# Two GNN layers on one core: fewer weights and q loads ahead of the attention loop, and another layout of the tiles that live longest there

## The chip, the cores and the metric

The kernel runs on one core of a Trainium2 chip. The metric is the device time of one execution in microseconds (us). TensorE appears in the profile as PE (and PEld for its weight loads), VectorE as DVE, ScalarE as ACT, GpSimd as POOL, SyncE as SP. SP, ACT and POOL can issue DMAs; "SPq" is SP's queue, "ACTq" that of ACT. L12 means line 12 of the kernel before.

## What is computed

There are 3327 nodes with 128 features, and a dense adjacency matrix. Cut to what matters:

```python
h = relu(layernorm(x))                                  # layer 0
agg = adj.T @ h / deg
x = x + relu(batchnorm(agg @ W_n.T + b_n + h @ W_c.T + b_c))

h = relu(layernorm(x))                                  # layer 1, n=3327, d=128, 8 features each
q = (h @ Wq.T).reshape(d, n, 8)                         # the same for k and v
a = einsum('dnh,dmh->dnm', q, k) * d**-0.5 + adj + adj
out = einsum('dnm,dmh->dnh', softmax(a, axis=2), v)
x = x + out.reshape(n, 8 * d) @ Wo.T
```

Layer 1 is 128 attentions over all 3327 nodes with eight features each; they are nearly all of the work.

## The kernel before

All instructions are placed by hand: each engine runs its own in the order of the program text, and the framework inserts the waits. Where a tile takes memory that an earlier tile held, its first user waits for the last users of the earlier one. Pools lie on a stack: pools opened after a closed one get its memory.

**Layer 0 (L286 to L598)**, about 300 us. The adjacency is read in 26 chunks (L412), and PE sums the seven `acc` banks. The nodes `x` live in `xs`, the normed nodes of layer 1, turned, in `B`; `A` and `C` are work tiles of the same size. All four are in the pool `l0`, `xs` first. Three chunks' buffers (`l0adj`) then take the last seven columns' worth of the transposed adjacency for the first three query blocks (`EARLY = 3`, L433). `weigh_early` (L439) turns such a buffer into weights exp(2 adj) with one ACT instruction and writes it to DRAM (`wd`). It runs twice beside the batch norm (L499) and once at the end (L598).

After the batch norm, `residual` adds the layer's output to `xs` for four chunks of nodes at a time and writes these to DRAM (`xd`); `stats` takes their layer-norm statistics. The first part of q, k and v is projected early (`project_now`, L567) and written to DRAM. SP then loads k (8 loads of 208 KB) and v, and ACT issues 16 loads of q (104 KB each, all 3328 columns). Then, in the order of the text: casts of k into place, alternately on POOL and ACT (L581); the rest of the residuals; `roots(4, NC)` on ACT (L591); the norms, turns and columns of layer 1 into `B`; `hd`, the write of `B` to DRAM (L597); the last `weigh_early`.

**Between (L647).** A pool `zero` with a small tile `zeros`, set by POOL and written by a POOL DMA behind the end of `att`.

**Layer 1, the loop (L652 to L869).** 32 batches `i` of four attentions, 7 blocks `y` of queries (six of 512, one of 255), 13 steps `s`: 2912 steps. A step handles four pieces of keys. For two or three of them ("plain") PE forms the scores, DVE adds the adjacency (L818, tile `d` from `at`, read from DRAM), ACT takes the exponential of all of them (L856). For one or two pieces ("rest") ACT takes the exponential straight from PSUM (L828) and POOL multiplies by the ready weights `wt` (L831, read from `wd`). PE then sums with v (L604), three steps later (`LAG`). `fetch` loads `at` (four buffers) and `wt` (three) two steps ahead.

In the first batch, `more_weights` (L734) makes the weights of block y + 1 during block y, but only from block 3 on (`y + 1 < EARLY` returns): four times a load `t`, an exponential on ACT a step later (L749) and a write to `wd` a step after that. `beside` runs further projections there, on PE, DVE and POOL, using the tile `ov`. From step 39 of the first batch the q, k and v of the next batch are loaded into the second set of tiles.

Of the kernel before, what the change touches and what calls it, by code (L numbers as in the profile page):

```python
# [9 lines left out]
F32 = mybir.dt.float32  # L10
# [5 lines left out]
PSUM = bass.MemoryType.PSUM  # L16
DRAM = bass.MemoryType.DRAM

N = 3327
D = 128  # L20
H = 8
P = 128
NC = 26
T = N * D
NP = NC * P
NB = 512
G = 4
# [4 lines left out]
WC = 19  # L32
CH = 4 * NP // D
NG = D // G
EARLY = 3

# [6 lines left out]
def tile_two_layer_gnn(  # L45
# [17 lines left out]
    nc = tc.nc  # L63
# [4 lines left out]
    blocks = [(n0, min(NB, N - n0)) for n0 in range(0, N, NB)]  # L68

    const = ctx.enter_context(tc.tile_pool(name="const", bufs=1))  # L70
# [6 lines left out]
    qT = dram.tile([2 * H, TP], F32, name="qT")  # L77
# [5 lines left out]
    att = dram.tile([TP, H], F32, name="att")  # L83

    wd = dram.tile([NC - WC, P, N], F32, name="wd")
    xd = dram.tile([NP, D], F32, name="xd")
# [9 lines left out]
    make_identity(nc, ident)  # L96
    ones = const.tile([P, P], F32, name="ones")
    nc.vector.memset(ones, 1.0)
    eps = const.tile([P, 1], F32, name="eps")
    nc.vector.memset(eps, EPS)  # L100
    wqk = [const.tile([P, H * D], F32, name=n) for n in ("wq", "wk", "wv")]
# [5 lines left out]
    low_half = const.tile([P, 2], F32, name="low_half")  # L107
# [18 lines left out]

    sets = [tile_set(x) for x in range(2)]

    def q_loads(q, p0, d):

        qs = qT[:, bass.ds(d * N, NP)].rearrange("(a h) n -> a h n", h=H)
        return [(q[p0 + i * H : p0 + (i + 1) * H].bitcast(F32), qs[i // 2]) for i in range(4)]

    def k_loads(k, p0, d, n0, n):
        cols = bass.ds(d * N + n0, n)
# [101 lines left out]
    def projections(wk, hj, j, quick, ov, factor):  # L237
        return [
            projection(wk, hj, j, s, e, quick, ov, factor) for s in (1, 0, 2) for e in range(2)
        ]  # L240
# [45 lines left out]
    with tc.tile_pool(name="l0", bufs=1) as l0, tc.tile_pool(  # L286
        name="l0adj", bufs=3
    ) as ap, tc.tile_pool(name="l0s", bufs=2) as sp, tc.tile_pool(
        name="l0p", bufs=1, space=PSUM
    ) as pp:  # L290
        xs = l0.tile([P, NC, D], F32, name="xs")
        A = l0.tile([P, NC, D], F32, name="A")
        B = l0.tile([P, NC, P], F32, name="B")
        C = l0.tile([P, NC, P], F32, name="C")
        A2, B2, C2 = (t.rearrange("p c d -> p (c d)") for t in (A, B, C))
        junk = l0.tile([P, N], mybir.dt.bfloat16, name="junk")
# [74 lines left out]
        def beside(x):  # L371

            if x < NQ:
                pt, cs = turned(x, A, aside)
                nc.scalar.copy(B[:, cs, :], pt)
            elif x < 2 * NQ:
# [35 lines left out]
        for c in range(NC):  # L412
            a = ap.tile([P, 7 * NB], F32, name="a")
# [15 lines left out]
            i = c - 2 * NQ - 5  # L429
            if 0 <= i < NQ - 2 and 4 * i + 4 <= c:  # L430
                spread(i)
        weights = []
        for y, (n0, w) in enumerate(blocks[:EARLY]):  # L433
            a = ap.tile([P, 7 * NB], F32, name="a")
            a7 = a.rearrange("p (c n) -> p c n", c=7)
            nc.sync.dma_start(a7[:, :, :w], adjr[:, WC:, n0 : n0 + w])
            weights.append((a7, n0, w))

        def weigh_early():  # L439
            a7, n0, w = weights.pop(0)  # L440
            nc.scalar.activation(a7[:, :, :w], a7[:, :, :w], AF.Exp, bias=low, scale=2.0)
            nc.sync.dma_start(
                wd[:, :, n0 : n0 + w].rearrange("c p n -> p c n"), a7[:, :, :w]
            )
# [6 lines left out]
        b = l0.tile([1, 6], F32, name="bound")  # L451
# [37 lines left out]
        for i, (n0, w) in enumerate(blocks):  # L489
            s = slice(n0, n0 + w)  # L490
            nc.vector.tensor_tensor(B2[:, s], acc[i][:, :w], B2[:, s], ALU.mult)
            nc.tensor.matmul(acc[i][:, :w], wn, B2[:, s], start=True, stop=True)
            if i >= 1:
                hidden(i - 1)
            if i in (0, 2):
                spread(NQ - 2 + i // 2)
            if i == 3:
                set_flag()
            if i in (4, 6):  # L499
                weigh_early()  # L500
        hidden(NQ - 1)
        nc.vector.bn_aggr(bmv, bst.rearrange("p i s -> p (i s)"))
# [9 lines left out]
        def relu(i):  # L512
            n0, w = blocks[i]
            s = slice(n0, n0 + w)
            nc.scalar.activation(A2[:, s], A2[:, s], AF.Relu, bias=shift, scale=scale)

        def residual(i):
            pt, cs = turned(i, A, acc[i])
            nc.vector.tensor_add(xs[:, cs, :], xs[:, cs, :], pt)
            nc.sync.dma_start(  # L520
                xd.rearrange("(c p) d -> p c d", p=P)[:, cs, :], xs[:, cs, :]
            )

        def second_norm(i, engine):

# [6 lines left out]
        def columns(i, scalar):  # L532
            pt, cs = turned(i, C, acc[i])
            if scalar:
                nc.scalar.activation(B[:, cs, :], pt, AF.Relu)
            else:
                nc.vector.tensor_scalar(B[:, cs, :], pt, 0.0, None, ALU.max)

        def keep_columns(i0, i1):
            s = slice(4 * i0 * P, min(NC, 4 * i1) * P)  # L540
            nc.sync.dma_start(hd[:, s], B2[:, s])

        ov0 = l0.tile([P, D, H + 1], F32, name="ov0")
        nc.gpsimd.memset(ov0, 1.0)

        def project_now(j, banks):
            todo = projections(sp, B2[:, j * CH : (j + 1) * CH], j, True, ov0, low_half[:CH, 1:2])
            for p, b in zip(todo, banks):
                drive(p, b)
            for p in todo:  # L550
                drive(p)
                drive(p)
# [16 lines left out]
        q, k, v = sets[0]  # L569
        ks = sets[1][1].rearrange("p c n -> p (c n)")  # L570
# [4 lines left out]
            nc.sync.dma_start(*args)  # L575
        for i in range(4, NQ):
            relu(i)
        for b in range(G):
            for args in q_loads(q, 32 * b, b):
                nc.scalar.dma_start(*args)  # L580
        for x, c in enumerate(range(0, NC, 4)):  # L581
            n = min(4, NC - c)
            (nc.scalar.copy if x % 2 else nc.gpsimd.tensor_copy)(
                k[:, c : c + n, :],
                ks.bitcast(F32).rearrange("g (p c) -> g c p", c=NC)[:, c : c + n, :],
            )
        for i in range(2, NQ):
            if i > 2:
                residual(i)
# [4 lines left out]
            second_norm(i, nc.gpsimd if i % 3 == 0 else nc.vector)  # L594
        for i in range(1, NQ):
            columns(i, i % 2 == 0)
        keep_columns(0, NQ)  # L597
        weigh_early()  # L598

# [41 lines left out]
    def rows_of(c):  # L643
        return min(P, N - c * P)


    with tc.tile_pool(name="zero", bufs=1) as zp:  # L647
        z = zp.tile([P, H], F32, name="zeros")
        nc.gpsimd.memset(z, 0.0)
        nc.gpsimd.dma_start(att[T:, :], z)  # L650

    def attention():  # L652


        with tc.tile_pool(name="adj", bufs=4) as ap, tc.tile_pool(
            name="adw", bufs=3
        ) as wp, tc.tile_pool(name="exd", bufs=4) as ep, tc.tile_pool(
            name="exf", bufs=5
        ) as fp, tc.tile_pool(
            name="res", bufs=2  # L660
        ) as rp, tc.tile_pool(name="wk", bufs=2) as wk, tc.tile_pool(
            name="wk1", bufs=1
        ) as wk1, tc.tile_pool(name="psc", bufs=3, space=PSUM) as psc, tc.tile_pool(
            name="pav", bufs=1, space=PSUM
        ) as pav:

# [1 line left out]
            avs2 = [pav.tile([P, NB], F32, name=f"av{x}") for x in range(2)]  # L668
            for av in avs2:
                nc.vector.memset(av, 0.0)  # L670
            ov = wk1.tile([P, D, H + 1], F32, name="ov")
            nc.gpsimd.memset(ov, 1.0)
            if True:
                steps = [
                    (i, y, s)
# [16 lines left out]
                for x, (i, y, s) in enumerate(steps):  # L692
                    n0, w = blocks[y]
# [4 lines left out]
                    c = pairs(s)[1][0][0]  # L698
# [30 lines left out]
                    return p  # L729

                waiting, ending, pending = [], [], []
                late = None

                def more_weights(i, y, s):  # L734

                    k, phase = s // 3, s % 3
                    if i or y + 1 >= len(blocks) or y + 1 < EARLY or k > 3:
                        return
                    n0, w = blocks[y + 1]
                    c = WC + 2 * k  # L740
                    n = min(2, NC - c)
                    if phase == 0:
                        have["w"] = wk.tile([P, 2, NB], F32, name="t4")
                        nc.sync.dma_start(
                            have["w"][:, :n, :w], adjr[:, c : c + n, n0 : n0 + w]
                        )
                    elif phase == 1:
                        a = have["w"][:, :n, :w]
                        nc.scalar.activation(a, a, AF.Exp, bias=low, scale=2.0)  # L749
                    else:  # L750
                        nc.sync.dma_start(
                            wd[c - WC : c - WC + n, :, n0 : n0 + w].rearrange("c p n -> p c n"),
                            have["w"][:, :n, :w],
                        )
# [44 lines left out]
                for x, (i, y, s) in enumerate(steps):  # L799
                    n0, w = blocks[y]  # L800
                    fetch(x + PRE)
                    k = x - i * SU * len(blocks) - FROM[i]
# [4 lines left out]
                    while pending and (total - len(pending)) * (SU * len(blocks) - FROM[i] - 4) <= k * total:  # L807
                        pending.pop(0)()
                    more_weights(i, y, s)
                    due = len(waiting) == LAG  # L810
                    plain, rest = pairs(s)
                    d = ep.tile([P, 3, 2, NB], F32, name="d")
# [251 lines left out]
```

## Time and profile before

| | us |
|---|---|
| median of 3 runs (10511.46 to 10516.91) | 10513.71 |
| the profiled execution, its own time | 10527.91 |
| its span, from first to last instruction | 10526.1 |
| core clock granted to TensorE, mean | 0.986 |
| DMA: mean rate over the span | 165 GB/s |

The page also divides the span into 40 slices of 263 us (each digit is a busy share in tenths). The first slice holds layer 0, the rest is the loop:

```profile
PE   7889999999999999999999999999999999999999
DVE  5789999999999999999999999999999999999998
ACT  4889999999999999999999999999999999999998
POOL 0667777777777777777777777777777777777776
```

Later quotations are of two kinds. Lines of groups give line, engine, operation and tiles, then count, busy time and mean ns, then idle time before them and what ended it. Lines of a timeline give start and duration in us, then the instruction; in brackets stands the idle time of the engine before it.

### The profile page before, as it was taken

What the parts mean: (1) busy time and instruction counts of PE and PEld (TensorE: products, weight loads), DVE (VectorE), ACT (ScalarE), POOL (GpSimd) and SP (SyncE); (2) the same over time, 40 slices, a digit from 0 to 9 for tenths busy, and PEclk for the clock granted to TensorE, in tenths of its full rate; (3) what the DMA queues carried; (4) which work ended last, traced back from release to release, by engine and by line L of the source; (5) the groups of instructions that cost most, each with busy time, mean ns of one, the idle gap of its engine ahead of it and who ended that gap; (6) DMA issues with size and microseconds to landing.
All of it is one profiled execution on the core that took longest, in us unless ns stands there. A gap on an engine that the chain in (4) does not pass through costs nothing. (4 is left out here: it accounts for less than half of the span.)

```text
span 10526.1 us, 186778 instructions
## 1 busy us (share of the span) xinstructions
PE 9922.7 (94%) x72399; PEld 2813.8 (27%) x72399; DVE 9714.9 (92%) x9949; ACT 9948.5 (95%) x6200; POOL 7497.1 (71%) x3868
## 2 busy tenths in 40 slices
PE   7889999999999999999999999999999999999999
PEld 3222222222222222222222222222222222222222
DVE  5789999999999999999999999999999999999998
ACT  4889999999999999999999999999999999999998
POOL 0667777777777777777777777777777777777776
PEclk8899999999999999999999999999999999999999
DMA  7655555555555555555555555555555555555554
GB/s 241 192 168 163 157 168 165 163 162 160 162 166 165 164 162 157 161 170 163 160 162 157 165 170 165 160 158 163 164 169 163 162 163 158 165 165 167 156 152 128
DMA packets 1115761, 1731.67 MB, mean 165 GB/s; under 512 B 198350, under 2 KB 441932, under 8 KB 1107180
## 3 DMA queue, kind: packets, MB, share of 16 engines
q1 hardware_dynamic: 1110478, 1713.99, 56.3%
q8 instruction: 568, 9.31, 0.4%
q10 hardware_dynamic: 4350, 5.64, 0.2%
q14 instruction: 333, 2.73, 0.1%
q0 software_dynamic: 32, 0.00, 0.0%
HBM read 1618.76 MB, written 100.53 MB: 163 GB/s over the span
## 5 line engine op out<-in xcount | busy, mean ns | idle before, releaser
L818 DVE SCALAR_TENSOR_TENSOR d<-at,s 128x1024 f32<-128x1024 f32 x8512 | 9204.3, 1138 | 642.7 <-PE s L725 406.2
L831 POOL TENSOR_TENSOR f<-f,wt 128x1024 f32<-128x1024 f32 (+1 forms) x3136 | 6983.8, 2235 | 2619.1 <-ACT f L828 2572.0
L856 ACT ACTIVATE d<-d 128x3072 f32<-128x3072 f32 (+1 forms) x2912 | 7372.9, 2532 | 73.4 <-DVE d L818 70.5
L604 PE MATMUL av<-d,v 128*9 128x512 f32 x34048 | 5528.5, 569 | 0.1
L725 PE MATMUL s<-q,k 32*128 32x512 f32 x23296 | 4280.7, 482 | 505.7 <-DVE d L818 218.0
L725 PEld LDWEIGHTS s<-q,k 32*128 32x128 f32 x23296 | 1773.9, 182 | 5829.2 <-DVE d L818 3312.2
L828 ACT ACTIVATE f<-s 128x1024 f32<-128x1024 f32 (+1 forms) x3136 | 3014.8, 970 | 313.8 <-PE s L725 252.3
L604 PE MATMUL av<-f,v 128*9 128x512 f32 x12544 | 2864.0, 571 | 0.0
L604 PEld LDWEIGHTS av<-d,v 128*9 128x9 f32 x34048 | 630.7, 88 | 1381.6 <-issue 1265.4
L604 PEld LDWEIGHTS av<-f,v 128*9 128x9 f32 x12544 | 310.6, 88 | 52.9 <-issue 41.0
L180 POOL CAST k<-ks 128x256 fp32r<-128x256 f32 x434 | 284.2, 655 | 0.0
L416 PE MATMUL acc<-a,A 128*128 128x512 f32 (+1 forms) x364 | 151.3, 568 | 24.0 <-ACT A L350 23.3
L619 PEld LDWEIGHTS av<-ident,avs 128*128 128x128 f32 (+1 forms) x864 | 121.1, 208 | 179.9 <-issue 178.8
L226 POOL TENSOR_TENSOR o<-pf,o 104x512 fp32r<-104x512 f32 x124 | 160.4, 1293 | 9.9
L619 PE MATMUL av<-ident,avs 128*128 128x128 f32 (+1 forms) x864 | 163.8, 311 | 0.6 <-DVE avs L612 0.6
L225 POOL CAST o<-pf 104x512 fp32r<-104x512 f32 x124 | 75.8, 611 | 115.3 <-DVE pf L224 59.8
L612 DVE COPY avs<-av 128x512 f32<-128x512 f32 (+1 forms) x224 | 144.2, 644 | 2.8 <-PE av L604 2.8
L423 DVE TENSOR_REDUCE amax<-a 128x1 f32<-128x3327 f32 x26 | 93.7, 3610 | 37.7 <-DMA a<-in_adj 37.7
L416 PEld LDWEIGHTS acc<-a,A 128*128 128x128 f32 x364 | 68.8, 192 | 108.8 <-issue 84.4
L420 ACT ACTIVATE junk<-a 128x3327 bf16<-128x3327 f32 x26 | 77.4, 2977 | 6.6 <-DMA a<-in_adj 6.5
L389 POOL TENSOR_TENSOR sq<-wk 128x512 f32<-128x512 f32 x2 | 2.1, 1040 | 102.3 <-PE aside L390 102.3
L629 DVE TENSOR_TENSOR oq<-av,ri 128x128 f32<-128x128 f32 (+1 forms) x224 | 64.1, 286 | 7.7
(120 smaller groups left out, 952.0 us busy)
## 6 DMA issues: line engine op xcount, KB each, us to landing
at<-in_adjT SPq DMA_DIRECT2D x1728, 512.0 KB
wt<-wd SPq DMA_DIRECT2D x1344, 256.0 KB
at<-in_adjT SPq DMA_DIRECT2D x288, 255.0 KB
ks<-kT SPq DMA_DIRECT2D x496, 104.0 KB
q<-qT SPq DMA_DIRECT2D x496, 104.0 KB
at<-in_adjT SPq DMA_DIRECT2D x192, 256.0 KB
a<-in_adj SPq DMA_DIRECT2D x26, 1663.5 KB
wt<-wd SPq DMA_DIRECT2D x224, 127.5 KB
```

The lines of the kernel that those rows point to most:

```text
L180: nc.gpsimd.tensor_copy(k[:, c : c + n, half * 64 : half * 64 + 64], ks.bitcast(F32).rearrange("g (p c) -> g c p", c=NC)[:, c : c + n, :],)
L226: nc.gpsimd.tensor_tensor(o[:CH, 1], f[:CH], o[:CH, 0].bitcast(F32), ALU.subtract)
L416: nc.tensor.matmul(acc[i][:, :w], A[:, c, :], a[:, n0 : n0 + w], start=(c == 0), stop=(c == NC - 1),)
L423: nc.vector.tensor_reduce(amax[:, c : c + 1], a[:, :N], AX.X, ALU.max, apply_absolute_value=True)
L604: nc.tensor.matmul(av[32 * b : 32 * b + H + 1, :w], tiles[2][:, b, c, :], e, start=first, stop=last,)
L612: nc.vector.tensor_copy(avs[:, :w], av[:, :w])
L619: nc.tensor.transpose(pt[:R, j, :], avs[:, j : j + (R - 1) * J + 1 : J], ident)
L725: nc.tensor.matmul(p[:, x, :we], k[rs, c, :], q[rs, n0 : n0 + we], start=True, stop=True,)
L818: nc.vector.scalar_tensor_tensor(d[:, j, :, :w], have[0, i, y, c // 2][:, c % 2, :w] .unsqueeze(1).to_broadcast([P, 2, w]), SAFE / 2, p[:, ...
L828: nc.scalar.activation(f[:, :, :w], p[:, :, :w], AF.Exp, scale=2.0)
L831: nc.gpsimd.tensor_tensor(f[:, :, :w], f[:, :, :w], have[1, i, y, c][:, :w].unsqueeze(1).to_broadcast([P, 2, w]), ALU.mult,)
L856: nc.scalar.activation(flat, flat, AF.Exp, scale=2.0)
```

## The change

Seven edits belong together.

1. `EARLY` goes: only block 0 gets its weights ahead of the loop (one `weigh_early`, at L499). `more_weights` makes those of blocks 1 and 2 in blocks 0 and 1 of the first batch.
2. ACT issues 16 q loads of 512 columns (16 KB each). The rest of the columns (2816, 88 KB each) is loaded by SP, two loads per step in the first eight steps of the loop.
3. The casts of k move from ahead of the residuals to the end of layer 0.
4. `xd` is written once, for all nodes, right before `hd`, in place of seven writes.
5. `xs` and `B` move to a pool `l0last` that lies last on the stack. The loop's pools are reordered so that `exd` and `res` lie there.
6. `zeros` becomes a constant tile, set and written out at the start; the pool `zero` goes.
7. `ov` becomes one constant tile for layer 0 and the loop, set once at the start.

The block size `NB` stays 512.

```diff
-EARLY = 3
...
+    ov = const.tile([P, D, H + 1], F32, name="ov")
+    nc.gpsimd.memset(ov, 1.0)
+    zeros = const.tile([P, H], F32, name="zeros")
+    nc.gpsimd.memset(zeros, 0.0)
+    nc.gpsimd.dma_start(att[T:, :], zeros)
...
-    def q_loads(q, p0, d):
-
-        qs = qT[:, bass.ds(d * N, NP)].rearrange("(a h) n -> a h n", h=H)
-        return [(q[p0 + i * H : p0 + (i + 1) * H].bitcast(F32), qs[i // 2]) for i in range(4)]
+    def q_loads(q, p0, d, n0=0, n=NP):
+
+        qs = qT[:, bass.ds(d * N + n0, n)].rearrange("(a h) n -> a h n", h=H)
+        return [
+            (q[p0 + i * H : p0 + (i + 1) * H, n0 : n0 + n].bitcast(F32), qs[i // 2])
+            for i in range(4)
+        ]
...
-        name="l0p", bufs=1, space=PSUM
-    ) as pp:
-        xs = l0.tile([P, NC, D], F32, name="xs")
+        name="l0last", bufs=1
+    ) as ll, tc.tile_pool(name="l0p", bufs=1, space=PSUM) as pp:
+
+
+        xs = ll.tile([P, NC, D], F32, name="xs")
         A = l0.tile([P, NC, D], F32, name="A")
-        B = l0.tile([P, NC, P], F32, name="B")
+        B = ll.tile([P, NC, P], F32, name="B")
...
-        for y, (n0, w) in enumerate(blocks[:EARLY]):
+        for y, (n0, w) in enumerate(blocks[:1]):
...
-            if i in (4, 6):
+            if i == 4:
                 weigh_early()
...
             nc.vector.tensor_add(xs[:, cs, :], xs[:, cs, :], pt)
-            nc.sync.dma_start(
-                xd.rearrange("(c p) d -> p c d", p=P)[:, cs, :], xs[:, cs, :]
-            )
...
-        ov0 = l0.tile([P, D, H + 1], F32, name="ov0")
-        nc.gpsimd.memset(ov0, 1.0)
...
         for b in range(G):
-            for args in q_loads(q, 32 * b, b):
+            for args in q_loads(q, 32 * b, b, 0, NB):
                 nc.scalar.dma_start(*args)
-        for x, c in enumerate(range(0, NC, 4)):
-            n = min(4, NC - c)
-            (nc.scalar.copy if x % 2 else nc.gpsimd.tensor_copy)(
-                k[:, c : c + n, :],
-                ks.bitcast(F32).rearrange("g (p c) -> g c p", c=NC)[:, c : c + n, :],
-            )
...
         for i in range(1, NQ):
             columns(i, i % 2 == 0)
+        nc.sync.dma_start(xd.rearrange("(c p) d -> p c d", p=P), xs)
         keep_columns(0, NQ)
-        weigh_early()
+        for x, c in enumerate(range(0, NC, 4)):
+            n = min(4, NC - c)
+            (nc.scalar.copy if x % 2 else nc.gpsimd.tensor_copy)(
+                k[:, c : c + n, :],
+                ks.bitcast(F32).rearrange("g (p c) -> g c p", c=NC)[:, c : c + n, :],
+            )
...
-    with tc.tile_pool(name="zero", bufs=1) as zp:
-        z = zp.tile([P, H], F32, name="zeros")
-        nc.gpsimd.memset(z, 0.0)
-        nc.gpsimd.dma_start(att[T:, :], z)
...
-        ) as wp, tc.tile_pool(name="exd", bufs=4) as ep, tc.tile_pool(
+        ) as wp, tc.tile_pool(name="wk", bufs=2) as wk, tc.tile_pool(
             name="exf", bufs=5
-        ) as fp, tc.tile_pool(
+        ) as fp, tc.tile_pool(name="exd", bufs=4) as ep, tc.tile_pool(
             name="res", bufs=2
-        ) as rp, tc.tile_pool(name="wk", bufs=2) as wk, tc.tile_pool(
-            name="wk1", bufs=1
-        ) as wk1, tc.tile_pool(name="psc", bufs=3, space=PSUM) as psc, tc.tile_pool(
+        ) as rp, tc.tile_pool(name="psc", bufs=3, space=PSUM) as psc, tc.tile_pool(
...
-            ov = wk1.tile([P, D, H + 1], F32, name="ov")
-            nc.gpsimd.memset(ov, 1.0)
...
+                others = [
+                    args for b in range(G)
+                    for args in q_loads(sets[0][0], 32 * b, b, NB, NP - NB)
+                ]
...
-                    if i or y + 1 >= len(blocks) or y + 1 < EARLY or k > 3:
+                    if i or y + 1 >= len(blocks) or k > 3:
                         return
...
                     more_weights(i, y, s)
+                    for args in others[:2]:
+                        nc.sync.dma_start(*args)
+                    del others[:2]
```

More of the change, by code (lines that the diff above doesn't have):

```diff
@@ L541, in keep_columns @@
             nc.sync.dma_start(hd[:, s], B2[:, s])
-        ov0 = l0.tile([P, D, H + 1], F32, name="ov0")
-        nc.gpsimd.memset(ov0, 1.0)
         def project_now(j, banks):
-            todo = projections(sp, B2[:, j * CH : (j + 1) * CH], j, True, ov0, low_half[:CH, 1:2])
+            todo = projections(sp, B2[:, j * CH : (j + 1) * CH], j, True, ov, low_half[:CH, 1:2])
             for p, b in zip(todo, banks):
```

## The prediction

> **What bounds the kernel now.** I read the page first, for the engines and the slices; then the windows, to see where the even part begins; then the timeline of the engines between 200 and 320 us, since the change touches that part; last the timeline of ACT in the first blocks of the loop.
>
> The page shows a kernel with three engines nearly full, and one group per engine that fills it:
>
> ```profile
> PE 9922.7 (94%) x72399; PEld 2813.8 (27%) x72399; DVE 9714.9 (92%) x9949; ACT 9948.5 (95%) x6200; POOL 7497.1 (71%) x3868
> L856 ACT ACTIVATE d<-d 128x3072 f32<-128x3072 f32 (+1 forms) x2912 | 7372.9, 2532 | 73.4 <-DVE d L818 70.5
> L828 ACT ACTIVATE f<-s 128x1024 f32<-128x1024 f32 (+1 forms) x3136 | 3014.8, 970 | 313.8 <-PE s L725 252.3
> ```
>
> ACT's two exponentials follow one another without a gap in a step of the loop (ACT's timeline has L828 at 406.54 and the next one at 410.10, so a full step is 3.56 us). In the loop ACT sets the pace, and what is added to ACT there is paid nearly one to one. The change leaves the steady loop alone. It acts on what lies ahead of the first step and on blocks 0 and 1 of the first of 32 batches. So I need two sums: how much earlier the first step starts, and what the first two blocks give back.
>
> Windows (us, then PE, PEld, DVE, ACT and POOL busy, clock, DMA share, GB/s) of the stretch ahead of the loop:
>
> ```profile
> 233.50:264.00 30.50, 0.66 (x4) 0.26 (x2) 6.72 (x38) 0.00 (x0) 0.01 (x1) 0.50 0.80 123
> 264.00:280.00 16.00, 4.98 (x22) 4.22 (x22) 6.14 (x21) 4.91 (x7) 7.08 (x10) 0.52 0.48 102
> 280.00:298.00 18.00, 1.72 (x8) 0.76 (x8) 1.29 (x3) 5.73 (x4) 1.93 (x3) 0.58 0.67 249
> ```
>
> For 64 us hardly any engine works. The timeline (start, duration, what; in brackets the idle time before and what ended it) says why:
>
> ```profile
> 233.49 18.34 SPq L573 DMA_DIRECT2D k<-kT  x8
> 233.77 36.48 ACTq L580 DMA_DIRECT2D q<-qT  x16
> 240.06 0.30 DVE L333 BATCH_NORM_AGGREGATE ln_mv<-ln_st 128x2 f32<-128x6 f32 x2
> 252.76 6.05 SPq L575 DMA_DIRECT2D v<-v  x3
> 270.30 3.25 ACT L583 CAST k<-k 128x512 fp32r<-128x512 f32 x3 [37.39 <-DMA xd<-xs]
> 273.45 0.31 ACT L338 ACTIVATE ln_sd<-ln_mv,eps 128x22 f32<-128x22 f32 x1
> ...
> 280.39 0.34 SPq L541 DMA_DIRECT2D hd<-B  x1
> 281.45 3.28 ACT L441 ACTIVATE a<-a,low_half 128x3584 f32<-128x3584 f32 x1
> 286.29 0.10 POOL L649 MEMSET zeros<- 128x8 f32 x1 [8.63 <-issue]
> 292.04 0.75 POOL L650 DMA_DIRECT2D att<-zeros  x1 [5.64 <-issue]
> 293.97 0.37 SPq L713 DMA_DIRECT2D at<-in_adjT  x1
> 298.15 2.35 DVE L818 SCALAR_TENSOR_TENSOR d<-at,s 128x1024 f32<-128x1024 f32 x2 [16.55 <-DMA at<-in_adjT]
> 300.27 1.02 ACT L828 ACTIVATE f<-s 128x1024 f32<-128x1024 f32 x1 [7.58 <-PE s L725]
> ```
>
> First knot: ACT issues 16 loads of q and needs 36.48 us for it; the root L338, whose statistics were ready at 240.36, is queued behind them and behind ACT's three casts of k, and runs at 273.45. Second knot: `hd<-B` goes out at 280.39; the POOL memset of `zeros`, which takes over the memory of `xs`, starts at 286.29, right when that transfer would be over (5.9 us; the profile says only "issue"), its DMA at 292.04, and the first `at` of the loop, which takes the memory of `zeros`, at 293.97. The wait view puts 8.1 us of SP down to `att<-zeros`. So the first add of the loop starts at 298.15.
>
> **What the Trainium skill says.** "DMA: Bandwidth & Descriptors", section "Issuing engines are not separate DMA queues": loads issued from ScalarE and SyncE run on the same 16 DMA engines and interleave. The trace agrees: the 16 q and 8 k loads share 123 GB/s while the DMA share is 0.80. "Queues, rings and completion order" in the same page says that one DMA is split over up to 16 rings, not always all; here q loads have 8 rows and k loads 16. No view here shows single DMA engines. "ScalarE: Activation LUTs", "What ACT_TABLE_LOAD costs": about 1283 ns, and the trace shows 1.28 us. "TensorE: Matmul & The Clock Gate", Part 1: after idling the array runs at half rate; the trace grants 0.50 to 0.58 in these windows. The start of the loop has that penalty before and after.
>
> **Part 1, up to the root L338.** One exponential of `weigh_early` (two took 6.46 us) leaves ACT in front of the batch-norm roots; the statistics it meets come at 213.45, so only some 0.6 us is won. Without one `wd` write (1792 KB) and three `xd` writes ahead of `kT`, ACT's waits for `kT<-o` (2.53 and 1.04 us) should shrink by about 0.4. The loads thus start 1 us earlier, at 232.5.
>
> The 16 q loads now carry 512 of 3328 columns: 16 KB, not 104. In 233.5 to 264 the core moved 123 GB/s x 30.5 us = 3.75 MB. What must pass now ahead of ACT's last issue is k (8 x 208 KB), v (468 KB) and q (256 KB): 2.44 MB. At the old rate that ends at 252; at 200 GB/s (a block of the loop with loads of this kind runs at 212) at 245; the floor is the statistics, 240. I take 247.5 for the root, since the last q loads were interleaved with the v loads before, and I expect ACT to wait for those. Gain 26 us (21 to 33). The casts of k, moved behind the columns, no longer stand in front of it.
>
> **Part 2, from the root to the first add.** Root to `hd` was 280.39 - 273.45 = 6.94 us (normalising, turning, columns), unchanged. From `hd` to the first add was 17.76 us. Gone from it are `zeros`, its DMA and POOL's `ov` memset; the last exponential and its `wd` write too (ACT's first L828 waited 6.93 us for that write). What is left: `hd` itself (5.9) and one `at` (4.2 from issue to add, 293.97 to 298.15). Wholly beside each other they cost 4.6, wholly in turn 10.1; the `at` is queued behind `hd` in the same rings but its fixed latency overlaps: 8.0. The `xd` write, now whole (1664 KB) in front of `hd`, can start when v is out, and has about 8 us; if it has not, it is in the 10.1. `xs` and `B` lie under `exd` and `res`; the third `d` comes 7 us after the first, when `hd` has landed, so I cost that wait at nothing.
>
> The casts: POOL's four (3.90) follow its norms, 4.2 + 3.9 = 8.1 us after the root; ACT's three (3.25) follow its columns, ending 9.9 after, then a table load 1.28: its first L828 ends at 12.2. The add comes at 14.9, so they are hidden by 2.7 us; k must land by about 250 for that. The first add: 247.5 + 6.9 + 8.0 = 262.4, and 35.7 us are won (29 to 45).
>
> **Part 3, what the loop gives back.** `more_weights` now also runs in blocks 0 and 1: per block three exponentials of 1.05 us (start to start) and one of 0.6, 3.76 us of ACT. The timeline shows the other part: the first of a block waits for its own load.
>
> ```profile
> 396.65 1.93 ACT L856 ACTIVATE d<-d 128x2048 f32<-128x2048 f32 x1
> 401.93 1.15 ACT L749 ACTIVATE t<-t,low_half 128x1024 f32<-128x1024 f32 x1 [3.34 <-DMA t<-in_adjT]
> ```
>
> The next block's stall is 4.07. The price as a whole is read from blocks, cut at the copies of `av`:
>
> ```profile
> 311.00:358.60 47.60, 45.96 (x314) 11.50 (x306) 44.78 (x40) 44.78 (x28) 35.06 (x18) 0.97 0.50 150
> 358.60:410.60 52.00, 48.05 (x318) 12.21 (x318) 46.67 (x46) 47.46 (x29) 37.06 (x18) 0.95 0.60 188
> 410.60:463.50 52.90, 48.39 (x326) 12.63 (x322) 46.44 (x45) 48.51 (x31) 32.16 (x14) 0.98 0.70 201
> ```
>
> The last two hold five exponentials (4.8) and two stalls (7.4), 12.2 us of ACT, and are 9.7 longer than twice the first: 79%. Block 1 then costs (3.76 + 3.7) x 0.79 = 5.9. In block 0 the first `t` is the eighth load of an empty loop: issued about 3.5 us after the first `at` and used 6.2 us later (395.69 to 401.93 above), it holds up the second L828, which came 6.3 us after the first `at`, by 3.4; in strict turn (3.3 MB at 254 GB/s, 13 us) by 6.7. I take 5, less 1.5 that ACT idled at 313 anyway: 3.5 + 3.76 = 7.3. The 16 rests of q (88 KB, two a step on SP, behind the fetches) ride in the shadow of `at` tiles that are fetched two steps ahead; they are needed 5 steps after the last: 1 us, bounds 0 and 6. Together 14.2 (8 to 22).
>
> **Sum.** -35.7 + 14.2 = -21.5 us. The profiled execution took 10527.9 (span 10526.1), 14 above the median of 10513.7; taken from the median: 10492. This case's own range is -37 (45 won, 8 back) to -7 (29 won, 22 back).
>
> **Rivals.** (a) *The transfers hold ACT anyway.* If k, v and `xd` go no faster without q, the root comes at 259 and the add at 273 or later with the casts behind k: 22 to 25 won at most, and with block 0 costing 20: about 10512. For it: k loads took 18.34 us to issue, POOL waited 62 us for k. Against: q took a third of the bytes. (b) *A starved start.* `t`, its `wd` write and the q rests double the DMA of block 0 (150 GB/s) to about 270, above the 254 seen at its start; if `at` comes late in each of eight steps by 2 us, 16 more go: 10508 to 10514. (c) *Slower: the rests of q tie the loop to the loads.* If a load into columns 512 onward waits for the matmuls that read columns 0 to 511, and these for it, each of eight steps pays one load, 4 to 6 us, and SP's fetches stand behind: 8 x 6 = 48, +26 net: 10540. It is slower by 0.2% from 5.4 us a step. For it: all is one tile. Against: PE turned the first rows of `C` at 274.74 while DVE still wrote others until 278.5, so waits follow parts of a tile. (d) *Not what it says.* The title speaks of blocks of 496 and 351; no line of the diff sets them, so 512 and 255 stay and I give it no time.
>
> **How the numbers follow.** A measurement of this kernel can tell about 0.2%, 21 us, from no change; my forecast lies on that bound. Chances: forecast 0.74 (0.42 beyond 21, 0.32 within), (a) 0.08, (b) 0.08, (c) 0.10. Faster 0.42, same 0.48, slower 0.10. The range 10478 to 10514 holds nearly all of the forecast's case and the middle of (a) and (b), and leaves out (c).
>
> **What would show it.** ACT's q issues should take 10 to 18 us, L338 run near 247, the first `at` go out right behind `hd`, the first L818 near 262. In block 0 the first L749 should show a stall of 3 to 7 us on its load, and the first three `av` copies be 55, 53 and 53 us apart at most. If PE L725 waits for q in the first eight steps, (c) is right; if L338 is past 255, (a).

## The result and the profile after

| | before | after |
|---|---|---|
| median, us | 10516.0 (12 runs) | 10506.1 (12 runs) |
| ratio, with its 95% interval | | 0.9989 (0.9981 to 0.9998) |
| span of the profiled execution, us | 10526.1 | 10509.5 |

The changed kernel is 9.9 us faster, 0.1%; by the interval, 2 to 20 us. The forecast was 21.5 us, just outside that interval, with a range that holds the result. The two profiles differ by 16.6 us, more than the medians: one profile alone is not the verdict.

The timeline of the changed kernel ahead of the loop (start, duration, what; in brackets the idle time before, and what ended it):

```profile
231.66 12.48 SPq L576 DMA_DIRECT2D k<-kT  x8
...
231.92 10.13 ACTq L584 DMA_DIRECT2D q<-qT  x16
...
242.38 0.31 ACT L347 ACTIVATE ln_sd<-ln_mv,eps 128x22 f32<-128x22 f32 x1 [11.30 <-DMA q<-qT]
...
247.12 0.41 SPq L595 DMA_DIRECT2D xd<-xs  x1
249.32 7.25 SPq L547 DMA_DIRECT2D hd<-B  x1
256.66 0.39 SPq L707 DMA_DIRECT2D at<-in_adjT  x1
...
253.46 3.92 POOL L599 CAST k<-k 128x512 fp32r<-128x512 f32 x4 [6.87 <-DMA k<-kT]
...
265.13 6.88 DVE L819 SCALAR_TENSOR_TENSOR d<-at,s 128x1024 f32<-128x1024 f32 x6 [14.60 <-DMA at<-in_adjT]
```

ACT's 16 issues take 10.13 us, not 36.48; the root runs at 242.38, not 273.45; the first add at 265.13, not 298.15. That is 33.0 us, and the loop gives two thirds back. Windows of the first batch, cut at the first add and then at the copies of `av` into `avs` (us, then PE, PEld, DVE, ACT and POOL busy, clock granted, DMA share, GB/s), changed kernel:

```profile
265.13:340.90 75.77, 60.98 (x346) 14.52 (x346) 57.80 (x51) 59.33 (x37) 43.99 (x21) 0.80 0.77 232
340.90:395.60 54.70, 49.56 (x322) 12.64 (x322) 46.96 (x46) 51.24 (x33) 36.99 (x19) 0.94 0.65 206
395.60:447.40 51.80, 47.67 (x322) 12.62 (x322) 46.38 (x46) 47.86 (x30) 32.01 (x14) 1.00 0.72 209
447.40:512.60 65.20, 56.68 (x320) 12.85 (x318) 47.43 (x46) 52.52 (x33) 39.35 (x21) 0.80 0.69 204
512.60:577.80 65.20, 54.48 (x324) 12.27 (x320) 47.65 (x45) 51.54 (x33) 39.81 (x24) 0.84 0.69 190
577.80:633.20 55.40, 47.09 (x326) 11.75 (x322) 42.30 (x45) 44.68 (x30) 31.69 (x17) 0.96 0.48 124
```

The first row answers to this one of the kernel before:

```profile
298.15:358.60 60.45, 55.84 (x346) 14.91 (x346) 56.45 (x50) 55.09 (x33) 44.13 (x21) 0.87 0.55 172
```

I call this first stretch "stretch 0". It is 15.3 us longer after the change, but only 4.2 us of that is work of ACT (59.33 - 55.09). The other 11 us is ACT waiting, while TensorE has a lower clock (0.80 for 0.87). It reaches some four steps into block 1, so it holds that block's first extra exponential too. The second row is block 1, 2.7 us longer than before.

The changed kernel's wait view of ACT (who waited for whom: us in total, times, longest), over the whole first batch:

```profile
ACT f L829 <- PE s L719: 38.4, 29, 4.0
ACT t L747 <- DMA t<-in_adjT: 29.8, 6, 11.5
```

The longest of the second kind is the first exponential of the loop:

```profile
271.69 1.15 ACT L747 ACTIVATE t<-t,low_half 128x1024 f32<-128x1024 f32 x1 [11.52 <-DMA t<-in_adjT]
```

Before, the second of these waits was 14.5 us in four. So there were two suspects for what the loop gave back: ACT's waits for the loads `t` (L747, the exponential of `more_weights`), and the rests of q, which share in raising the traffic of stretch 0 from 172 to 232 GB/s.

### The profile page after: what moved, and what is told of

It is laid out like the page before. It is cut to its first block, busy times and chain, and to the rows that moved or that the text cites. A ratio compares the mean times of both kernels' runs of the same rounds, so it can differ in the third digit from the quotient of the medians.

```text
span 10509.5 us, 186813 instructions
## 1 busy us (share of the span) xinstructions
PE 9924.0 (94%) x72399; PEld 2811.7 (27%) x72399; DVE 9718.2 (92%) x9949; ACT 9949.8 (95%) x6206; POOL 7476.2 (71%) x3867
## 5 line engine op out<-in xcount | busy, mean ns | idle before, releaser
L425 PE MATMUL acc<-a,A 128*128 128x512 f32 (+1 forms) x364 | 152.5, 572 | 23.6 <-ACT A L359 23.6
L232 POOL CAST o<-pf 104x512 fp32r<-104x512 f32 x124 | 75.6, 610 | 116.0 <-DVE pf L231 58.5
```

What stands on the lines that cost most here:

```text
L425: nc.tensor.matmul(acc[i][:, :w], A[:, c, :], a[:, n0 : n0 + w], start=(c == 0), stop=(c == NC - 1),)
```

## The experiments

The table gathers what the profiles gave (us; "first add" is counted from the start of the span; the blocks are lengths between copies of `av`; "end" is the copy that closes the first batch, so it holds everything in which the kernels differ). What follows it, from there to the last copy of `av` in batch 32, took 9813 to 9826 us in every profile. Medians are set against the kernel before on the same chips.

| kernel | first add | stretch 0 | blocks 1 to 5 | end | median (before) | ratio (95%) |
|---|---|---|---|---|---|---|
| before | 298.2 | 60.5 | 51.9 52.9 62.4 62.2 58.8 | 680.2 | | |
| before again | 295.3 | 60.2 | 51.4 52.7 60.4 64.9 56.6 | 674.8 | | |
| after | 265.1 | 75.7 | 54.7 51.8 65.2 65.3 55.4 | 667.5 | 10506.1 (10516.0) | 0.9989 (0.9981 to 0.9998) |
| after again | 265.8 | 74.6 | 57.1 52.5 62.0 63.1 57.7 | 665.7 | | |
| e1, rests later | 264.8 | 73.5 | 56.5 53.2 59.5 66.0 58.6 | 665.2 | 10506.5 (10514.7) | 0.9994 (0.9988 to 1.0001) |
| e2, two blocks early | 266.1 | 70.5 | 54.2 52.7 61.6 66.1 58.5 | 662.7 | 10497.0 (10514.7) | 0.9984 (0.9977 to 0.9990) |
| e3, exponentials later | 265.1 | 70.9 | 50.0 50.5 53.6 57.7 53.8 | 635.6 | 10480.8 (10514.7) | 0.9963 (0.9950 to 0.9977) |
| e4, `xd` on ACT | 268.1 | 74.9 | 55.1 53.9 65.5 65.3 55.4 | 672.4 | 10507.9 (10514.7) | 0.9992 (0.9984 to 1.0001) |
| e5, e2 + e3 | 265.9 | 64.7 | 50.5 50.6 54.1 58.6 53.4 | 631.5 | 10473.8 (10513.5) | 0.9961 (0.9947 to 0.9975) |
| e6, before + e3's edit | 292.2 | 60.3 | 48.3 50.5 53.8 60.3 53.4 | 652.4 | 10492.7 (10516.3) | 0.9978 (0.9968 to 0.9987) |
| e7, whole q | 283.1 | 67.7 | 53.2 53.4 62.4 63.2 61.1 | 677.2 | 10511.4 (10516.3) | 0.9996 (0.9988 to 1.0004) |
| e8, whole q and rests | 277.6 | 73.5 | 55.8 52.5 65.5 65.2 55.4 | 678.6 | | |
| e9, q on SP | 268.7 | 74.3 | 56.1 52.8 61.1 66.1 58.6 | 670.8 | 10505.8 (10513.5) | 0.9992 (0.9984 to 1.0000) |
| e10, e5 + e9 | 269.2 | 65.1 | 50.5 50.7 54.1 59.4 53.6 | 637.8 | 10471.5 (10513.5) | 0.9958 (0.9944 to 0.9972) |

**Do the block times repeat?** Both kernels were profiled once more.

> The kernel before, profiled a second time, to see how far the block times of one profile repeat. Stall theory (block times follow from the order of the work): the first add within 1 us of 298.15, the stretch from it to the first copy of av within 2 us of 60.45, the next five blocks within 2 us of 51.9, 52.9, 62.4, 62.2 and 58.8. Rival (TensorE's half-clock windows fall by chance and carry several us a block): single blocks differ by more than 4 us.

> The changed kernel, profiled a second time. Stall theory: first add within 1 us of 265.13, the stretch to the first copy of av within 2 us of 75.8, the next five blocks within 2 us of 54.7, 51.8, 65.2, 65.3 and 55.4. Rival (chance): single blocks differ by more than 4 us, and the 15.3 us that block 0 gave back is partly luck of one execution.

Stretch 0 repeats within 1.2 us in both kernels. Single blocks move by up to 3.2 us, more than the theory allowed and less than the rival wanted, and the first add of the kernel before moved by 2.8. e6 below has the same text ahead of the loop as the kernel before, and its first add is at 292.2: with whole q loads the front moves by 6 us in three profiles. With the small loads it repeats better (264.8 to 265.8 in both profiles of the changed kernel, e1 and e3). Ends are thus good to some 5 us, and stretch 0 is the sharpest measure (60.5, 60.2 and 60.3 in the three). The mean ends of the two pairs, 677.5 and 666.6, are 10.9 us apart, like the medians.

**e1: the rests of q later in block 0.**

```diff
-                    for args in others[:2]:
-                        nc.sync.dma_start(*args)
-                    del others[:2]
+                    for args in others[:4] if x >= 6 else []:
+                        nc.sync.dma_start(*args)
+                    if x >= 6:
+                        del others[:4]
```

> The changed kernel with the 16 loads of the rest of q issued four per step in steps 6 to 9 of the first block, not two per step in steps 0 to 7. In the changed kernel the stretch from the first add to the first copy of av takes 75.8 us, 60.45 before. Stall theory (ACT waits for the first load t, and what follows from that): t is issued ahead of the rests, so the stall in front of the first L747 stays within 1.5 us of 11.5 us and the stretch stays at 73 to 78 us. Contention theory (the rests of q crowd the loads of the first steps): the stretch falls to 62 to 67 us and the whole by about 10 us.

Stretch 0 fell by 1 to 2 us only, and ACT's wait in front of the first L747 stayed (10.5 us). The stall theory held here, and the median gained nothing (8.2 us below the kernel before, where the changed kernel has 9.9). But this says only that the place of the rests inside block 0 matters little, not that the rests are free.

**e2: the weights of block 1 ahead of the loop again.**

```diff
-        for y, (n0, w) in enumerate(blocks[:1]):
+        for y, (n0, w) in enumerate(blocks[:2]):
...
-            if i == 4:
+            if i in (4, 6):
                 weigh_early()
...
-                    if i or y + 1 >= len(blocks) or k > 3:
+                    if i or y + 1 >= len(blocks) or y + 1 < 2 or k > 3:
```

> The changed kernel with the weights of block 1 made ahead of the loop again, by a second exponential beside the batch norm; block 0 of the loop makes none. Stall theory: the first add comes at most 2 us later than the 265.1 of the changed kernel, and the stretch from it to the first copy of av falls from 75.8 to 60 to 64 us, near the 60.45 before; the whole is 10 to 14 us below the changed kernel. Contention theory: the rests of q are still there, the stretch stays above 68 us and the whole gains under 7 us.

The front came within the 2 us allowed (266.1). The median is 17.6 us below the kernel before, 7.7 better than the changed kernel's 9.9; the two intervals overlap, and 7.7 lies between the two theories. Stretch 0 stayed at 70.5, where the stall theory wanted 60 to 64. Part of the miss is my accounting: stretch 0 still holds block 1's first exponential with its stall, which the ACT timeline of this run shows to be 3.79 + 1.05 us. The other 5 us had to come from something else than block 0's weights.

**e7 and e8: what the rests cost, and what they save.** e7 loads q whole on ACT ahead of the loop; e8 does that and issues the rests in the loop all the same, so that they bring the same numbers a second time.

```diff
-            for args in q_loads(q, 32 * b, b, 0, NB):
+            for args in q_loads(q, 32 * b, b):
                 nc.scalar.dma_start(*args)
```

(in e7 the list `others` and its loop are gone as well)

> The changed kernel with q loaded whole by ACT ahead of the loop again; no rests in the loop. If the q loads held ACT, as the prediction has it: ACT's 16 issues take 25 to 36 us again, the root comes at 257 to 268 instead of 242.4, the first add at 275 to 288 instead of 265.1. In block 0: if the rests of q cost several us there, the stretch from the first add to the first copy of av falls from 75.8 to 66 to 70 us; if the stall at the first t is all of it, it stays at 73 to 76. The whole: 0 to 12 us above the changed kernel.

> e7_whole_q with the 16 loads of the rests of q issued in the loop's first eight steps as well (they bring the same numbers once more). Front as in e7: first add at 281 to 285. Rests theory (their traffic in block 0 costs 5 to 8 us): the stretch from the first add to the first copy of av is 73 to 77 us, as in the changed kernel (75.8 and 74.6), not the 67.7 of e7. Rival (the longer stretch comes of the earlier start of the loop, with other traffic still under way): 66 to 69 us.

The front is what the prediction's first step says: with q whole, ACT issues for 30.84 us and the root comes at 264.16.

```profile
233.00 30.84 ACTq L584 DMA_DIRECT2D q<-qT  x16
264.16 0.31 ACT L347 ACTIVATE ln_sd<-ln_mv,eps 128x22 f32<-128x22 f32 x1 [31.98 <-DMA q<-qT]
```

e8 has the same text ahead of the loop, but its root came at 259.94 and its first add at 277.6, earlier than expected. Against the mean of the two profiles of the changed kernel, 265.5, the small loads thus win 12 to 18 us of the first add. In stretch 0 the rests cost 73.5 - 67.7 = 5.8 us (e8 against e7, one profile each), or 7.5 if the mean of the two profiles of the changed kernel is set against e7; e8 is in the range of the rests theory. The way in which they cost is only half seen. No engine shows a wait for a late `at` or `wt` in stretch 0, and PE none for q:

```profile
PE s L719 <- DVE d L819: 16.1, 23, 5.4
PE s L719 <- ACT f L829: 2.7, 2, 1.8
```

(the wait view of PE in the changed kernel, 265 to 341 us, whole). ACT's exponentials waited for PE at 293.66, 302.68 and 309.05, in and behind stretches where TensorE ran at half clock, as windows of the changed kernel show:

```profile
282.00:289.00 7.00, 5.95 (x42) 1.47 (x38) 5.64 (x6) 7.00 (x6) 3.71 (x2) 0.99 0.83 243
289.00:296.00 7.00, 5.78 (x28) 1.14 (x30) 3.61 (x3) 5.05 (x4) 3.60 (x2) 0.51 0.88 231
...
306.00:310.00 4.00, 4.00 (x22) 0.55 (x20) 2.72 (x3) 1.31 (x3) 1.74 (x3) 0.57 0.02 7
```

ACT was busy for the full 7.00 us of the first row and idle for 2 of 7 in the second. ACT's waits for PE in stretch 0 add up to nothing in e7, 4.0 us in e8 and 6.0 us in the changed kernel, so the cost shows there. What leads from the loads to these waits and to the half clock stays open.

**e3 and e6: the exponential two steps after its load.** The load `t` is issued in step 0, 3, 6, 9 of a block; its exponential moves from the next step to the one after, and the write to `wd` to the step after that. Same work, same blocks. e6 is the same edit in the kernel before.

```diff
-                    if i or y + 1 >= len(blocks) or k > 3:
+                    if i or y + 1 >= len(blocks) or k > 4:
...
                     if phase == 0:
...
+                        if k > 0:
+                            nc.sync.dma_start(
+                                wd[c - 2 - WC : c - WC, :, n0 : n0 + w].rearrange("c p n -> p c n")
...
+                        if k < 4:
+                            have["w"] = wk.tile([P, 2, NB], F32, name="t4")
...
-                    elif phase == 1:
+                    elif phase == 2 and k < 4:
```

> The changed kernel with each exponential of more_weights two steps after the issue of its load instead of one, and the write to wd one step after that. Same work in the same blocks. Stall theory: the waits of 3 to 4 us in front of L747 at each block's start vanish, that of the first block shrinks by 3 us or more, blocks 1 to 5 get 2 to 3 us shorter each, the stretch up to the first copy of av falls to 66 to 71 us, and the whole is 12 to 22 us below the changed kernel. Rival (the exponentials themselves, 3.76 us of ACT a block, set the price, and the waits only take idle time): blocks stay within 1 us, the whole gains under 5 us.

> The kernel before with its exponentials of more_weights two steps after their loads instead of one, as in e3_exp_later. If the waits of ACT in front of these exponentials, and what TensorE's clock makes of them, are what the blocks lose: blocks 2 to 5 come down from 52.9, 62.4, 62.2 and 58.8 to within 2 us of the 50.5, 53.6, 57.7 and 53.8 of e3, the whole is 18 to 26 us below the kernel before, and e3 stays 10 to 20 us below this one (33 us of front less 8 to 15 of weights and rests of q). Rival (the late exponential pays only together with the change): gain under 8 us.

This is the largest effect of the study: 24 us in the changed kernel (33.9 us below the kernel before, where the changed kernel has 9.9), more than the 12 to 22 expected, and 23.6 us in the kernel before. Windows of e3, stretch 0 to block 3:

```profile
265.07:336.00 70.93, 58.80 (x346) 14.63 (x346) 57.02 (x50) 59.64 (x37) 43.92 (x21) 0.84 0.84 236
336.00:386.00 50.00, 46.87 (x322) 12.38 (x320) 46.50 (x45) 49.74 (x31) 37.06 (x18) 1.00 0.70 227
386.00:436.60 50.60, 46.74 (x322) 12.15 (x320) 46.48 (x46) 50.29 (x32) 33.24 (x14) 1.00 0.74 213
436.60:490.20 53.60, 47.64 (x320) 12.17 (x318) 46.92 (x46) 51.52 (x33) 38.27 (x21) 1.00 0.86 256
```

and e3's wait view of ACT:

```profile
ACT f L832 <- PE s L719: 31.9, 24, 7.1
ACT t L755 <- DMA t<-in_adjT: 4.6, 4, 2.6
```

ACT's waits for `t` fall from 29.8 to 4.6 us. Blocks 1 to 5 get 4.7, 1.3, 11.6, 7.5 and 1.6 us shorter than in the first profile of the changed kernel, where 2 to 3 each were expected; it is 26.7 us in all, against either profile. The waits for `t` that lie in these blocks were 14.5 us (four of 3.0 to 4.1) and are 1.0 now. So the stalls themselves are about half of what the blocks won. The rest goes with the clock: block 3 has nearly the same busy time of ACT (52.52 and 51.52), lost one stall of 4.1 us and got 11.6 us shorter (8.4 against the second profile), and the clock column goes from 0.80 (0.89) to 1.00.

Chance is no rival here: block 3 takes 53.6 to 54.1 us at clock 1.00 in all four kernels with this edit (e3, e5, e6, e10), and 59.5 to 65.5 us at 0.79 to 0.95 in the ten profiles without it. The edit also moves the write to `wd`, which waits on SP for the exponential; SP waits 59.6 us for it in the first batch of the changed kernel and 58.5 us in e3, so a freer SP is not the reason.

Not all of it is cured. e6's block 4 missed its expectation and stayed slow, with a wait for `t` of only 0.3 us:

```profile
505.00:565.40 60.40, 53.07 (x320) 12.95 (x320) 47.56 (x46) 50.75 (x32) 39.83 (x23) 0.89 0.66 187
```

The Trainium skill, "TensorE: Matmul & The Clock Gate", Part 1, says that a recent lack of work halves the array's clock. The traces agree in part: in block 3 the half clock goes when ACT's stalls go (0.80 to 1.00), in block 4 of e6 it stays without them (0.89). Nor does it follow at once: in the changed kernel the last stall ahead of the row of block 3 ends at 440.6, the clock is still 1.00 up to 456, and 0.50 from 460 to 468. The chain from the stall to the half clock is not shown.

Whether the change is worth more without these stalls is not shown either. The medians of e3 and e6, less their references, are 10.3 us apart (33.9 and 23.6), as far as the changed kernel and the kernel before are (9.9). The ends are 16.8 apart, against 10.9, but each is good to some 5 us only.

**e4 and e9: what ends the front now.** In the changed kernel `hd` needs 7.25 us to issue, right behind `xd` on SP. e4 issues `xd` on ACT, e9 issues the 16 small q loads on SP (each a change of the engine's name in one line).

> The changed kernel with the one write of xd issued on ACT's queue instead of SP's. In the changed kernel the write of hd, issued right behind it on SP, takes 7.25 us to issue and the first at goes out at 256.66. If the full queue of SP is the cause: hd takes under 1 us to issue, the first at goes out at 250 to 251, the first add comes at 258 to 262 instead of 265.1, the whole gains 3 to 7 us. Rival (the bytes of xd and hd ahead of it set the time, not the issue): the at goes out early but lands no earlier, the first add stays at 264 to 266, no gain.

> The changed kernel with the 16 small q loads issued by SP behind k and v, not by ACT. If ACT's q issues are still what the root waits for: ACT runs the root right after its statistics, at 238 to 239.5 instead of 242.4, hd goes out 3 to 4 us earlier, and since the k loads are no longer spread between q loads, k lands by 247 to 250 instead of 253; the first add comes at 257 to 262 instead of 265.1; the whole gains 3 to 8 us. Rival (the bytes of k, v, xd and hd ahead of the first at set its landing): root early, first add still at 263 to 266.

Both missed: the first add came 3 us later in both, and neither median gains (6.8 and 7.6 us below the kernel before, where the changed kernel has 9.9). In e4 `hd` did not go out before 259.95, since SP waited for `xd` to land (11.6 us in front of `hd` by its wait view). So the theory of the full queue is not tested. But the run shows what `xd` does:

```profile
249.20 0.41 ACTq L595 DMA_DIRECT2D xd<-xs  x1
259.95 0.37 SPq L547 DMA_DIRECT2D hd<-B  x1
```

With `xd` out of the way, `hd` takes 0.37 us to issue and the first add follows 8.2 us behind it. In e8, where `xd` goes out 16 us ahead of `hd`, it is 8.2 us too:

```profile
253.24 0.41 SPq L595 DMA_DIRECT2D xd<-xs  x1
269.41 0.35 SPq L547 DMA_DIRECT2D hd<-B  x1
```

In e7 (17 us ahead) it is 9.5. In the two profiles of the changed kernel, with `xd` only 2 us ahead of `hd`, it is 15.8 and 16.0. In e9 the root did come early (239.78), but SP, held by q's issues for 11.17 us, sent `xd` at 254.69 and `hd` at 255.20, and the add came 13.5 us behind `hd`:

```profile
238.88 3.76 SPq L578 DMA_DIRECT2D v<-v  x3
243.40 11.17 SPq L584 DMA_DIRECT2D q<-qT  x16
254.69 0.41 SPq L595 DMA_DIRECT2D xd<-xs  x1
255.20 3.99 SPq L547 DMA_DIRECT2D hd<-B  x1
```

Windows of the changed kernel fit the rival, that the bytes set the time:

```profile
231.50:242.00 10.50, 0.39 (x2) 0.00 (x0) 6.89 (x39) 0.00 (x0) 0.00 (x0) 0.50 0.53 124
242.00:249.50 7.50, 4.90 (x22) 4.14 (x22) 6.46 (x21) 1.89 (x4) 3.19 (x6) 0.60 1.01 151
249.50:265.00 15.50, 2.18 (x8) 0.96 (x8) 0.97 (x2) 5.57 (x5) 3.92 (x4) 0.56 1.05 319
```

From 242 on the DMA engines are full (shares 1.01 and 1.05). What stands in front of the first `at` is then k, v, `xd` and `hd`. That fewer bytes there would bring the add forward was not tried.

**e5 and e10: all together.**

> e3_exp_later with the weights of block 1 made ahead of the loop as in e2. If ACT's time alone is left as the price of these weights (three exponentials of 1.05 us and one of 0.6): 3 to 5 us below e3, the stretch from the first add to the first copy of av falls from 70.9 to 66 to 68. Rival (the loop's start is held by the rests of q, and the exponentials fill time that is idle anyway): within 2 us of e3.

> e5 and e9 together: two blocks' weights ahead, exponentials two steps after their loads, small q loads on SP. If the gains add up: 30 to 42 us below the changed kernel, 42 to 52 us below the kernel before. Rival (they overlap, since the loop's start is held by traffic): no more than 3 us below e5.

e5 is 40 us faster than the kernel before (10473.8 and 10513.5), 0.9961 (0.9947 to 0.9975), and clearly faster than the changed kernel. Its end is 4.1 us ahead of e3's, as ACT's time alone says; stretch 0 fell by 6.3, more than the 3 to 5 expected, which left out that e3 still waits 3.7 us for `t` in block 0. e5 also prices the rests a second time: its stretch 0 has them, but no exponential of block 0's and no wait for `t`, and is 4.3 us longer than before. Less some 0.8 for block 1's first exponential, that is an estimate of 3.5 us, so part of the 5.8 to 7.5 above may come of rests and stalls together. e10's median (42.0 us below the kernel before, 2.4 below e5) lies in the ranges of both theories; its first add is 3.3 us later than e5's and its end 6.3, so the profile shows no gain of e9's edit. The medians do not tell e3, e5 and e10 apart; by the end of the first batch e5 is ahead.

## Why the prediction was right in sign and range, and too large

- **The q loads hold the root.** Right, and shown by e7. ACT's issue was put at 10 to 18 us and took 10.13; the root was put at 247.5 and came at 242.4.
- **From the root to `hd`, 6.94 us.** Right: 242.38 to 249.32.
- **From `hd` to the first add, 8.0 us, at most 10.1.** The failed term of the front: 15.8 us (249.32 to 265.13). The failed step is `xd`, put at nothing because it would have about 8 us ahead of `hd`. It went out at 247.12, about when the prediction let it (8 us ahead of 254.4), but the early root brought `hd` 2.2 us behind it, into DMA engines that were full. Where `xd` had 11 to 17 us (e4, e8, e7) the term was 8.2 to 9.5, as forecast. k landed at 253.4, later than the 250 it was allowed, but the casts stayed hidden: ACT's ended at 256.7, POOL's at 257.4. That the first add came at 265.1 for 262.4 is luck: the root was 5.1 us early, this term 7.8 late.
- **The front.** 31.3 us on the means of two profiles (296.7 and 265.5), for 35.7; part of the difference is that the kernel before starts its loop earlier on the mean than in the one profile I had (298.2).
- **The weights of blocks 1 and 2 in the loop.** ACT's work was there as described. The stall of the first L749 was to be 3 to 7 us and shows as 11.5, but most of that ACT waits anyway: in e2, with no `t` in block 0, it waits 7.1 us for PE at this place. The exponential behind it comes 7.6 us after the first add, 2.1 in e2; less the 1.05 of the exponential of `t` itself, the stall holds the loop up by 4.5 us, and the prediction reckoned with 3.4 to 6.7. Block 0 with weights and no rests (e7) has a stretch 0 of 67.7, 7.4 us over the 60.3 before; the sum had 7.3 for block 0, and of block 1's 5.9 some 3.8 falls into this stretch (its first exponential and stall, 4.75 x 0.79). That term was too large by 3.7 us.
- **The rests of q, 1 us with bounds 0 to 6.** The failed step of the loop: 5.8 to 7.5 us. The reasoning, that `at` is fetched two steps ahead and covers them, holds (no wait for `at`), but the cost came another way. Block 1 lost 4.2 us (means of two profiles: 55.9 and 51.7) where 2.1 were left in the sum. Loop in all: 20.4 us for 14.2, within the 8 to 22 given.
- **What would show it.** The first two copies of `av` after stretch 0 came 54.7 and 51.8 us apart, as said (57.1 and 52.5 in the second profile), the third 65.2 (62.0) for 53 "at most": that was a slip, since this block took 62.4 before.
- **Sum.** -31.3 + 20.4 = -10.9 us, measured by the ends of the first batch; -21.5 predicted. Both parts erred the same way, by 4.4 and 6.2 us, and the wide range held them.
- **Rivals.** (a) is out: the root was not late. (The prediction's ground against it was itself off: q was 1664 of the 3796 KB of k, v and q, 44%, not a third.) (b), a starved start, named the right place, but `at` was never late. (c) is out: PE shows no wait for q in stretch 0. (d): the file sets no new block size, and blocks 0 to 6 are as wide as before.

## What to carry to other kernels

Loads that an engine issues stand in front of everything behind them in its program (16 loads of q held ACT for 36.48 us, small ones for 10.13). So load ahead of a loop only what the first steps read, and look which engine issues it. A large write that the loop does not need can still cost when it goes out right ahead of what the loop needs: with `xd` close ahead of `hd`, the way from `hd` to the first add took 16 us, not 8. Where an instruction of the pacing engine uses a load, put another step between issue and use before counting bytes: here that one move was worth more than twice the whole change. And judge a gain ahead of a loop by the time at which the loop's first unchanged part ends, not by the first instruction of the loop.

## What was not expected of the hardware

- Waits of ACT of 3 to 4 us a block seem to cost more than their length: 14.5 us of them in the kernel before cost 23.6 us by the medians (14 to 34 by the interval) and 20 to 22 in blocks 1 to 5, while the granted clock of block 3 rose from 0.89 to 1.00 when they were gone.
- One write of 1664 KB in pieces of 512 bytes (26 x 128 of them) was followed on the same queue, 2.2 us later, by an issue that took 7.25 us (3.99 in e9); with 16 us or more between them it took 0.34 or 0.35 (e7, e8). Why is open.
- Loads that no engine is seen to wait for cost 5.8 us in 73 when they run beside the loop's first steps (e8 against e7).
